# Measured durations in the planner's costs, gathered tiles in pieces of at most 512, and another first graph, in a four-layer graph network

## The chip, the cores and the metric

The kernel runs on one core of a Trainium2 chip. A core has TensorE (PE in the profile; PEld is its weight load), VectorE (DVE), ScalarE (ACT), GpSimd (POOL), and SyncE (SP), which issues transfers. The metric is the device time of one execution in microseconds; a kernel's time is the median of its runs. The profile is of one execution.

## The reference, cut to what matters

Sixteen graphs of 1024 nodes with 64 features, a dense weighted adjacency `adj` (16, 1024, 1024) with about nine entries per row, four layers, each with a norm ahead of it and a residual around it:

```python
def reference(x, adj, nodemask, ...):
    # each layer: h = max(layernorm(x), 0); x = x + layer(h)
    # layer 0: (adj @ h) @ W.T
    # layer 1: m = relu(relu(h @ W1 + b1) @ W2 + b2); msg = relu(adj @ m); GRU gates of (msg, h):
    #          (1 - z) * n + z * h
    # layer 2: T0 = h, T1 = adj @ T0, T2 = 2 * adj @ T1 - T0;  (T0*K0 + T1*K1 + T2*K2) @ weight + bias
    # layer 3: thin out the neighbour lists of nodes with more than 10 neighbours, both ways;
    #          agg = 0.25*quantile_0.25 + 0.5*quantile_0.5 + 0.25*quantile_0.75 over the neighbours,
    #          per feature (sort, then interpolate);  relu((h + agg) @ W1 + b1) @ W2 + b2, times the mask
```

## The kernel before

**Chains and the planner.** The work is written as generators, called chains, that yield one operation after another. `Weave.run` (line 430) is a list scheduler: of all chains it takes the operation that can start first by its reckoning, within 0.1 us the one of the chain with the smallest key, and issues it. The reckoning takes each operation's duration from `Line.cost` (line 304), a formula per engine. The order so found is kept on each engine by order dependencies, so an engine works its operations off in planned order, whatever really comes first. All operations of the chains are issued in line 301, so the profile's lines say L301 and are told apart by the names of their tiles.

**Chains and keys.** `transposing` loads the eight blocks (512 KB each) of a graph's adjacency by SP's queue, transposes them on PE into the tiles `AT` (15 of them, a stock shared by all graphs), key b - 2.5. The first eight blocks have places of their own: two tiles `block`, and six pieces of the two gather buffers `G`. `coding` (key b - 2) takes the sign of the transposed blocks on ACT into `there`, and PE multiplies it with fixed powers of two into `code`, 64 words per node that hold which neighbours there are. `listing` (key b - 1.5) first turns the node mask (a copy on DVE and a transposition on PE) and then unpacks each graph's code to a list of up to 24 neighbours per node, on DVE (`max`, `match_replace`, names `more`, `top`, `cand`, `L`). Two chains of `layering` (key b - 3) work even and odd graphs: `layers` computes layers 0 to 2. Layers aggregate with `into` (line 907: PE, `bank<-AT,nodes`, names of the tiles). Gates of layer 1 are products with `wg`; `of_h` and `hn` (lines 994 and 1012) are their steps on DVE. Layer 2 ends with a product with `wca` that is added to `X` (line 1058). Then `layers` waits for the list and writes a row per node into `pay`: list, counts, mask, and the last norm's features. SP stores them to `table` and `rows` in DRAM (lines 1075 and 1077).

**Norms.** `norm` (line 879) sums on DVE (`st`), squares on ACT per 128 nodes with an accumulator (`sq`, eight instructions, each with an instruction that reads the accumulator), takes the root on ACT (`sd`) and the reciprocal on DVE (`ri`), and scales on ACT per 128 nodes.

**Gathers and quantiles.** `gathering` (key b + 1) has POOL gather, per graph, 10 neighbour slots x 8 groups of 128 nodes = 80 indirect transfers (line 622) from `table` into a buffer `G`, 64 features and two numbers per row. There are two buffers `G`; a buffer is free again when PE has read the sorted slots for the quantiles. `quantiling` sorts on DVE: `hits` and `bad` find dropped neighbours, a `scalar_tensor_tensor` puts them at infinity, and a network of `min` and `max` sorts the 11 slots, partly into the tile `net`. Then `coef` weighs the slots, PE sums them (`bank<-G,c`), and `dense` does the last MLP (`yo`, `h`), key b. After all graphs, nodes with longer lists are gathered again in four groups (`MANY`, with up to 23 slots), at the end of the program.

**Width.** A slot of a graph has 8 x 64 = 512 elements per partition. `parts` (line 1147) cuts an operation over several slots in pieces of at most

```python
few = max(1, int(LONGEST / (T * C)))
```

slots, here two: 1024 elements. `coef`'s products take at most `few` slots as well (line 1218).

Of the kernel before, what the change touches and what calls it, by code (L numbers as in the profile page):

```python
# [16 lines left out]
AF = mybir.ActivationFunctionType  # L17
ALU = mybir.AluOpType
AX = mybir.AxisListType
# [3 lines left out]
P = 128  # L23
N = 1024
NT = N // P
# [76 lines left out]
GATHER = 1.33  # L102
RANK = 3.0
SHARE = 3
LONGEST = 1024
AT = 15
LIST_KEY = -1.5
CODE_KEY = -2
# [177 lines left out]
class Line:  # L286
# [15 lines left out]
        return op  # L302

    def cost(self, method, out, reads, kwargs):
        n = max(a.free_size() for a in [out] + reads)
        extra = "accum_out" in kwargs
        if self.name == "DVE":
            fixed = {"match_replace": 0.27, "max": 0.16}.get(method, 0.155)
            return fixed + n / 960 + 0.08 * extra, 0.0
        if self.name == "ACT":  # L310
            scalars = sum(hasattr(kwargs.get(k), "ap") for k in ("bias", "scale"))
            return 0.225 + n / 1400 + 0.09 * scalars + 0.19 * extra, 0.0
        if self.name == "PE":
            if method == "transpose":
                return 0.12, 0.25
            n = out.free_size()
            if n == NB and mybir.dt.size(reads[0].dtype) == 2:
                return 0.12, 0.3
            pair = n == 512 and reads[0].shape[0] == P and out.shape[0] == C
            return (0.46 if pair else max(0.22, 0.06 + n / 545)), 0.3  # L320
        if self.name == "SP":
            return 0.4, 2.0 + out.nbytes() / 150e3
        return 1.33, 2.2


class Weave:
# [16 lines left out]
    def give(self, name, t):  # L343
        self.stocks[name].append(t)
# [121 lines left out]
class Fast:  # L466
# [4 lines left out]
    def __init__(self, tc, half, whole, weights):  # L471
# [93 lines left out]
        self.weave = weave = Weave(tc)  # L565
        self.T, self.V, self.S = Line("PE", nc.tensor), Line("DVE", nc.vector), Line("ACT", nc.scalar)
        self.G, self.D = Line("POOL", nc.gpsimd), Line("SP", nc.sync)
        self.take = {}
        weave.leash = None, None

# [64 lines left out]
    def listing(self, nodemask):  # L635
        V = self.V
        mf, mu8 = self.small("h1", (P, 512))[:, 0:P], self.small("h1")[:, P:2 * P].bitcast(U8)[:, 0:P]
        yield self.D.dma_start(mu8, nodemask.rearrange("b (t p) -> (b t) p", p=P))
        yield V.tensor_copy(mf, mu8)
        bank = yield "q"  # L640
        yield self.T.transpose(bank[:, 0:P], mf, self.ident)
        self.mask = self.small("mask", (P, P))
        yield V.tensor_copy(self.mask, bank[:, 0:P])
        self.weave.give("q", bank)
        for b in range(GRAPHS):
            yield float(b) + LIST_KEY
            yield from self.lists(b)
        yield float(GRAPHS) - RANK
        yield from self.longest()

    def coding(self):

        V, T, S = self.V, self.T, self.S
        for b in range(GRAPHS):
            yield float(b) + CODE_KEY
            bank = yield "bits"
            yield T.matmul(bank.rearrange("p (t w) -> p t w", w=NB), self.ones16[0:1, 0:P],
                           self.low[0:1, None, :].to_broadcast([1, NT, NB]), start=True, stop=False)
            turned = self.turned[b]
            for j in range(0, NT, 2):  # L660
                there = yield "there"
                for i in range(2):
                    yield lambda: len(turned) > j + i
                    yield S.activation(there[:, i, :], turned[j + i], AF.Sign)
                self.masked[b] = j + 2
                own = there.rearrange("p i (t m) -> p (i t) m", m=P)[:, j:j + NT + 2:NT + 1, :]
                yield V.tensor_mul(own, own, self.noteye[:, None, :].to_broadcast([P, 2, P]))
                for i in range(2):
                    for t in range(NT):
                        yield T.matmul(bank[:, t * NB:(t + 1) * NB], there[:, i, t * P:(t + 1) * P],  # L670
                                       self.bits[:, (j + i) * NB:(j + i + 1) * NB], start=False,
                                       stop=j + i == NT - 1 and t == NT - 1)
                self.weave.give("there", there)
            code = yield "code"
            yield S.activation(code.rearrange("p t w -> p (t w)"), bank, AF.Copy, scale=1.0 / UNIT)
            self.weave.give("bits", bank)
            self.coded[b] = code
# [167 lines left out]
    def transposing(self, adj):  # L845

        D, T, S = self.D, self.T, self.S
        blocks = {}


        early = self.early

        def load(i):
            b, j = divmod(i, NT)
            blocks[i] = block = early.pop(0).rearrange("p (t m) -> p t m", m=P) if 2 <= i < NT else (yield "block")
            yield D.dma_start(block, adj[b, :, j * P:(j + 1) * P].rearrange("(t p) m -> p t m", p=P))

        total = GRAPHS * NT
        yield -1.0
        for i in range(NT):  # L860
            yield from load(i)
        for i in range(total):
            b, j = divmod(i, NT)
            yield float(b) - 2.5
            if NT <= i + 1 < total:
                yield from load(i + 1)
            block = blocks.pop(i)
            at = yield "AT"
            for half in range(2):
                bank = yield "tp"  # L870
                for q in range(4):
                    yield T.transpose(bank[:, q * P:(q + 1) * P], block[:, 4 * half + q, :], self.ident)
                yield S.activation(at[:, 512 * half:512 * half + 512], bank, AF.Copy)
                self.weave.give("tp", bank)
            if not 2 <= i < NT:
                self.weave.give("block", block)
            self.turned[b].append(at)

    def norm(self, w, h, X, then=None):

        V, S = self.V, self.S
        st, va, sd, ri, off = (self.small(f"{name}{w}") for name in ("st", "va", "sd", "ri", "off"))
        yield V.tensor_reduce(st, X, axis=AX.X, op=ALU.add)
        yield V.tensor_scalar(st, st, -1.0 / C, None, op0=ALU.mult)
        sq = self.small(f"sq{w}", (P, C))
        for t in range(NT):
            yield S.activation(sq, X[:, t, :], AF.Square, bias=st[:, t:t + 1], accum_out=va[:, t:t + 1])
        yield S.activation(sd, va, AF.Sqrt, bias=self.eps, scale=1.0 / C)
        yield V.reciprocal(ri, sd)
        yield V.tensor_mul(off, st, ri)  # L890
        for t in range(NT):
            yield S.activation(h[:, t, :], X[:, t, :], AF.Relu, bias=off[:, t:t + 1], scale=ri[:, t:t + 1])
            if then:
                yield from then(t)

    def layers(self, w, b, x):
# [10 lines left out]
        def into(bank, h, last=False):  # L907

            def step(j):
                if j == 0:  # L910
                    yield lambda: len(turned) > 0
                yield lambda: len(turned) > j
                for half in range(2):
                    yield T.matmul(bank[half * C:(half + 1) * C, :], h[:, j, :], turned[j][:, cols[half]],
                                   start=j == 0, stop=not last and j == NT - 1)
                if last:
                    yield lambda: self.masked[b] > j
                    give("AT", turned[j])
            return step
# [10 lines left out]

        h = yield "nodes"
        bank = yield "fm"
        yield from self.norm(w, h, X, into(bank, h))
        self.turns += 1
        wide = yield "wide"
        aggT = wide[0:C, :]
# [15 lines left out]
        def turn(t):  # L952
# [3 lines left out]
            if t % 4 == 3:  # L956
                yield S.activation(cat[0:C, cols[t // 4]], turned_h[-1][0:C, :], AF.Copy)
                give("fm", turned_h[-1])
        yield from self.norm(w, h, X, turn)
        aug = yield "wide"  # L960
        for half in range(2):
            bank = yield "fm"
# [57 lines left out]

        h = yield "nodes"
        bank = yield "fm"
        yield from self.norm(w, h, X, into(bank, h))
        wide = yield "wide"
        t1 = wide[0:C, :]
        for half in range(2):
# [21 lines left out]
                yield T.matmul(both[half * C:(half + 1) * C, t * P:(t + 1) * P], h[:, 4 * half + t, :], self.k02,  # L1048
                               start=False, stop=t == 3)
        give("nodes", h)  # L1050
        aug = yield "wide"
        for half in range(2):
            yield S.activation(aug[0:C, cols[half]], both[half * C:(half + 1) * C, :], AF.Copy)
        give("fm", both)
        bank = yield "fm"
        o = yield from by_node(bank, aug[0:C, :], self.wca, self.bcr)
        give("wide", aug)
        yield V.tensor_add(X, X, o)
        give("fm", bank)


        yield lambda: b in self.listed
        L, notes = self.listed[b]
# [6 lines left out]
                              op0=ALU.mult, op1=ALU.add)  # L1070
        give("L", L)
        give("notes", notes)
        yield from self.norm(w, pay[:, :, H:H + C], X)
        table = self.table[b * STRIDE:b * STRIDE + N, :].rearrange("(t p) c -> p t c", p=P)
        yield self.store(b, "table", table, pay[:, :, H:H + R])
        rows = self.rows[b * N:(b + 1) * N, :].rearrange("(t p) w -> p t w", p=P)
# [870 lines left out]
```

## Time and profile before

| | |
|---|---|
| median of 5 runs | 3383.01 us (3376.92 to 3401.72) |
| profiled execution | 3376.92 us, its span 3375.0 us |
| mean granted TensorE clock | 0.67 |
| instructions | 24102 |
| DMA | 141 MB, 42 GB/s over the span |
| gathers of line 622 | 1402, 997 ns each |
| first gather | 160.9 us |

The span runs from the first instruction to the last. In the views, L301 is a line, `G<-net` means that a tile `G` is written from a tile `net` (buffer numbers are left out), x is a count, and "idle before" is the time in which the engine stood still just before, with what released it ("remote" is a semaphore from elsewhere, "issue" a wait for nothing that the profile shows).

### The profile page before, as it was taken

The page shows a single profiled execution, that of the slowest core. Times are in us where ns is not written, and L with a number is a line of the kernel's source. Part 1 is how long each engine was busy: PE and PEld are TensorE (multiplying, and loading weights), DVE is VectorE, ACT ScalarE, POOL GpSimd, SP SyncE. Part 2 cuts the span into 40 slices and gives each one's busy share as a digit, 9 for nine tenths or more (in the row PEclk, how much of TensorE's full clock was granted, in tenths as well). Part 3 has the DMA queues.
Part 4 walks back from the last instruction along what each step waited for, and adds up shares of the span by engine and source line. Part 5 has one row for each costly group of instructions (what it writes and reads, how often), then busy time and mean ns, then how long its engine had stood idle before and what let it go on. Part 6 is the DMA issues. An engine that isn't in the chain of part 4 may idle for free. (4 is left out here: it accounts for less than half of the span.)

```text
span 3375.0 us, 24102 instructions
## 1 busy us (share of the span) xinstructions
PE 1744.6 (52%) x7024; PEld 803.7 (24%) x7024; DVE 1548.3 (46%) x3675; ACT 1093.9 (32%) x3002; POOL 1427.5 (42%) x1441
## 2 busy tenths in 40 slices
PE   6726455381746547273846645482745476333222
PEld 3302112130313223131413212230312232111121
DVE  2212136271725436171725436271725346395846
ACT  5504234260615234151614324260614234111100
POOL 1070624526061634526171534427071534527774
PEclk8858567595767667585767657585767677555555
DMA  3212222221212212222312212221211121111110
GB/s 84 60 27 53 45 46 50 37 62 25 63 31 54 46 30 62 31 51 30 76 26 47 44 32 50 39 65 26 67 26 39 42 38 25 19 21 27 26 29 16
DMA packets 246841, 141.00 MB, mean 42 GB/s; under 512 B 76048, under 2 KB 223952, under 8 KB 246704
## 3 DMA queue, kind: packets, MB, share of 16 engines
q1 hardware_dynamic: 199824, 90.21, 11.0%
q0 software_dynamic: 46096, 48.62, 10.1%
q8 instruction: 59, 0.97, 0.1%
q14 instruction: 78, 0.64, 0.1%
q10 hardware_dynamic: 784, 0.57, 0.1%
HBM read 120.12 MB, written 19.17 MB: 41 GB/s over the span
## 5 line engine op out<-in xcount | busy, mean ns | idle before, releaser
L622 POOL DMA_INDIRECT G<-table,pay x1402 | 1397.2, 997 | 1899.2 <-DVE net L301 1169.9
L301 PE MATMUL bank<-AT,nodes 128*64 128x512 f32 x2048 | 614.8, 683 | 116.1 <-issue 65.4
L301 PE MATMUL bank<-wide,wg 64*64 64x512 f32 (+1 forms) x192 | 119.6, 708 | 325.4 <-ACT wide L301 284.5
L301 PE MATMUL bank<-G,c 128*128 128x512 f32 (+3 forms) x382 | 196.0, 634 | 163.5 <-DVE G L301 98.5
L301 PEld LDWEIGHTS bank<-AT,nodes 128*64 128x64 f32 x2048 | 159.8, 153 | 421.9 <-issue 298.0
L301 PE MATMUL bank<-c,block 128*128 128x128 f32 x976 | 229.6, 365 | 18.9 <-ACT AT L301 8.1
L301 ACT ACTIVATE wide<-bank 64x512 f32<-64x512 f32 x128 | 75.6, 590 | 494.2 <-remote 362.2
L301 ACT ACTIVATE sq<-pay,st 128x64 f32<-128x64 f32 x512 | 177.7, 347 | 103.2 <-DVE st L301 87.4
L301 PE MATMUL bank<-of_h,m 64*128 64x512 f32 (+2 forms) x72 | 61.5, 949 | 284.8 <-issue 232.2
L301 DVE TENSOR_TENSOR hn<-nodes,bank 128x256 f32<-128x256 f32 x32 | 13.4, 419 | 421.4 <-remote 250.1
L301 ACT ACTIVATE AT<-bank 128x512 f32<-128x512 f32 x256 | 150.0, 589 | 158.7 <-PE bank L301 123.8
L301 DVE SCALAR_TENSOR_TENSOR of_h<-bank,bhn,wide 64x512 f32<-64x512 f32 x32 | 23.8, 744 | 382.0 <-PE bank L301 268.7
L301 DVE MAX8 L<-cand 128x8 f16<-128x103 f16 x384 | 92.3, 263 | 229.8 <-remote 136.2
L301 PEld LDWEIGHTS bank<-c,block 128*128 128x128 f32 x976 | 152.9, 187 | 169.3 <-issue 137.9
L301 DVE TENSOR_TENSOR G<-G 128x1024 f32<-128x1024 f32 (+7 forms) x215 | 187.4, 902 | 2.2
L301 PE MATMUL bank<-m,h 128*128 128x64 f32 x274 | 68.1, 407 | 218.6 <-ACT h L301 206.6
L301 ACT ACTIVATE nodes<-pay,off,ri 128x64 f32<-128x64 f32 x384 | 153.5, 429 | 24.1 <-DVE off L301 14.8
L301 DVE TENSOR_TENSOR net<-G 128x1024 f32<-128x1024 f32 (+7 forms) x140 | 140.3, 1032 | 3.2 <-PE bank L301 2.2
L301 PEld LDWEIGHTS bank<-G,c 128*128 128x128 f32 x382 | 72.6, 235 | 273.9 <-issue 154.7
L301 ACT ACTIVATE G<-G,coef 128x64 f32<-128x64 f32 x384 | 95.2, 337 | 128.3 <-DVE coef L301 128.2
L301 ACT ACTIVATE there<-AT 128x1024 f16<-128x1024 f32 x128 | 132.4, 1046 | 0.4
L301 PEld LDWEIGHTS bank<-m,h 128*128 128x128 f32 x274 | 59.1, 305 | 268.4 <-ACT h L301 219.3
(188 smaller groups left out, 2605.9 us busy)
## 6 DMA issues: line engine op xcount, KB each, us to landing
block<-in_adj SPq DMA_DIRECT2D x122, 512.0 KB
G<-table,pay POOLq DMA_INDIRECT x1402
rows<-pay SPq DMA_DIRECT2D x16, 632.0 KB
table<-pay SPq DMA_DIRECT2D x16, 264.0 KB
pay<-in_x SPq DMA_DIRECT2D x16, 256.0 KB
out<-yo SPq DMA_DIRECT2D x16, 256.0 KB
G<-in_adj SPq DMA_DIRECT2D x6, 512.0 KB
c<-in_half ACTq DMA_DIRECT2D x1, 246.0 KB
```

Of the source, the lines that this page charges most:

```text
L301: return Op(self, lambda: f(*args, **kwargs), writes, reads, cost, later)
L622: return self.nc.gpsimd.indirect_dma_start(out=out, out_offset=None, in_=table, in_offset=bass.IndirectOffsetOnAxis(ap=at, axis=0))
```

## The change

Four parts. (1) `Line.cost` gets other durations for PE and DVE, and a transfer has the same cost on every queue. The planner then finds another order for all engines. (2) `LONGEST` is 512: with graphs of 8 x 64 elements per slot, every operation on gathered tiles takes one slot. (3) For graph 0: `norm` has a form with five DVE operations over all 1024 nodes (`early`) in place of the squares and scalings on ACT; every second one of the first eight blocks is issued on ACT's queue (`self.A`); the mask's turn waits for graph 0's code, and coding for the end of graph 0's first aggregation (`self.turns > 0`). (4) For all graphs, the last product of layer 2 comes behind the list's columns of `pay`.

```diff
-LONGEST = 1024
+LONGEST = 512
...
     def cost(self, method, out, reads, kwargs):
+        if method == "dma_start":
+            return 0.4, 2.0 + out.nbytes() / 150e3
...
-            fixed = {"match_replace": 0.27, "max": 0.16}.get(method, 0.155)
+            fixed = {"match_replace": 0.145, "max": 0.155}.get(method, 0.155)
...
             if method == "transpose":
-                return 0.12, 0.25
+                return 0.19, 0.25
             n = out.free_size()
             if n == NB and mybir.dt.size(reads[0].dtype) == 2:
-                return 0.12, 0.3
+                return 0.075, 0.3
             pair = n == 512 and reads[0].shape[0] == P and out.shape[0] == C
-            return (0.46 if pair else max(0.22, 0.06 + n / 545)), 0.3
-        if self.name == "SP":
-            return 0.4, 2.0 + out.nbytes() / 150e3
+            return (0.58 if pair else max(0.34, 0.06 + n / 545)), 0.3
         return 1.33, 2.2
...
+        self.A = self.S
...
         yield self.D.dma_start(mu8, nodemask.rearrange("b (t p) -> (b t) p", p=P))
+        yield lambda: 0 in self.coded
         yield V.tensor_copy(mf, mu8)
...
             yield float(b) + CODE_KEY
+            yield lambda: self.turns > 0
             bank = yield "bits"
...
-            yield D.dma_start(block, adj[b, :, j * P:(j + 1) * P].rearrange("(t p) m -> p t m", p=P))
+            queue = self.A if i % 2 and i < NT else D
+            yield queue.dma_start(block, adj[b, :, j * P:(j + 1) * P].rearrange("(t p) m -> p t m", p=P))
...
-    def norm(self, w, h, X, then=None):
+    def norm(self, w, h, X, then=None, early=False):
...
+        if early:
+            yield V.tensor_add(h, X, st[:, :, None].to_broadcast([P, NT, C]))
+            square = yield "nodes"
+            yield V.tensor_mul(square, h, h)
+            yield V.tensor_reduce(va, square, axis=AX.X, op=ALU.add)
+            self.weave.give("nodes", square)
+            yield S.activation(sd, va, AF.Sqrt, bias=self.eps, scale=1.0 / C)
+            yield V.reciprocal(ri, sd)
+            yield V.scalar_tensor_tensor(h, h, 0.0, ri[:, :, None].to_broadcast([P, NT, C]), op0=ALU.max, op1=ALU.mult)
+            for t in range(NT):
+                if then:
+                    yield from then(t)
+            return
...
-        yield from self.norm(w, h, X, into(bank, h))
+        yield from self.norm(w, h, X, into(bank, h), early=b == 0)
...
-        aug = yield "wide"
-        for half in range(2):
-            yield S.activation(aug[0:C, cols[half]], both[half * C:(half + 1) * C, :], AF.Copy)
-        give("fm", both)
-        bank = yield "fm"
-        o = yield from by_node(bank, aug[0:C, :], self.wca, self.bcr)
-        give("wide", aug)
-        yield V.tensor_add(X, X, o)
-        give("fm", bank)
-
 
         yield lambda: b in self.listed
...
         give("L", L)
         give("notes", notes)
-        yield from self.norm(w, pay[:, :, H:H + C], X)
+
+        aug = yield "wide"
...
+        yield V.tensor_add(X, X, o)
+        give("fm", bank)
+
+
+        yield from self.norm(w, pay[:, :, H:H + C], X, early=b == 0)
```

The other calls of `norm` in `layers` get `early=b == 0` too.

More of the change, by code (lines that the diff above doesn't have):

```diff
@@ L958, in turn @@
                 give("fm", turned_h[-1])
-        yield from self.norm(w, h, X, turn)
+        yield from self.norm(w, h, X, turn, early=b == 0)
         aug = yield "wide"
@@ L1022, in layers @@
         bank = yield "fm"
-        yield from self.norm(w, h, X, into(bank, h))
+        yield from self.norm(w, h, X, into(bank, h), early=b == 0)
         wide = yield "wide"
@@ L1072, in layers @@
         give("notes", notes)
-        yield from self.norm(w, pay[:, :, H:H + C], X)
+        aug = yield "wide"
+        for half in range(2):
+            yield S.activation(aug[0:C, cols[half]], both[half * C:(half + 1) * C, :], AF.Copy)
+        give("fm", both)
+        bank = yield "fm"
+        o = yield from by_node(bank, aug[0:C, :], self.wca, self.bcr)
+        give("wide", aug)
+        yield V.tensor_add(X, X, o)
+        give("fm", bank)
+        yield from self.norm(w, pay[:, :, H:H + C], X, early=b == 0)
         table = self.table[b * STRIDE:b * STRIDE + N, :].rearrange("(t p) c -> p t c", p=P)
```

## The prediction

> **What bounds the kernel now.** I read the engines' busy times first, then the waits of POOL, then busy time by stretches, then the timelines inside one graph.
>
> ```profile
> PE 1744.6 (52%) x7024; PEld 803.7 (24%) x7024; DVE 1548.3 (46%) x3675; ACT 1093.9 (32%) x3002; POOL 1427.5 (42%) x1441
> ```
>
> No engine is over 52%, so the time is a chain of waits. POOL's gathers (line 622) come in streams of 80 per graph, which makes them a good clock:
>
> ```profile
> POOL G L622 <- DVE net L301: 1169.9, 15, 99.7
> POOL G L622 <- PE bank L301: 143.5, 16, 84.3
> POOL G L622 <- DMA table<-pay: 143.2, 1, 143.2
> ```
>
> POOL waits 1169.9 us in 15 pieces, some 80 us each, for DVE to finish an older graph's network, and once 143.2 us for the first table. From the timeline of POOL, the first gather is at 160.9 us, stream 2 starts at 544.5 and stream 15 at 3008.7: 13 cycles of 189.6 us on average. One cycle in detail, from 1487.3 (columns: start:end, length, busy us and count of PE, PEld, DVE, ACT, POOL, then clock, DMA share, GB/s):
>
> ```profile
> 1530.00:1550.00 20.00, 0.00 (x0) 0.00 (x0) 0.00 (x0) 0.00 (x0) 14.89 (x16) 0.50 0.15 27
> ...
> 1605.00:1676.00 71.00, 55.76 (x277) 27.32 (x277) 54.53 (x89) 50.23 (x138) 0.02 (x1) 0.76 0.30 66
> ```
>
> The reader is to see two limits. While gathers run (1487 to 1596), there are stretches where PE, DVE and ACT all stand still: hand-offs between them arrive late. Adding the gaps of 5 us and more over the whole span gives 583 us in 32 stretches. After the stream, DVE works through 71 us (54.5 busy, and 13 us in gaps of over 0.4 us, where it waits for ACT and PE; 9 us in the graph before), while POOL does nothing. Between the two lies the end of the gated unit of the next graph, `hn` (line 1012):
>
> ```profile
> 1554.88 1.21 ACT L301 ACTIVATE wide<-bank 64x512 f32<-64x512 f32 x2 [46.91 <-remote]
> ```
> ```profile
> 1601.57 0.42 DVE L301 TENSOR_TENSOR hn<-nodes,bank 128x256 f32<-128x256 f32 x1 [14.10 <-remote]
> ```
>
> The second half of `hn` follows at 1603.61, 116.3 us after the stream's start; over streams 2 to 13 it comes 113 to 120 after it, on average 117.6. Then the DVE phase runs to the next stream. So: cycle = time to `hn` + DVE phase.
>
> **First graph.** Durations are from the timelines of before. (a) PE stands still until 23.8, for the node mask:
>
> ```profile
> 23.79 0.48 PE L301 MATMUL bank<-c,h 128*128 128x128 f32 x1 [8.12 <-DVE h L301]
> ```
>
> The new wait moves the mask's copy and transposition behind graph 0's coding, and coding behind layer 0. From 24.06 to 51.4 PE transposes and aggregates eight blocks, 3.4 us each, 0.5 of it coding's eight small matmuls of 0.07, which now come later. From 15 us on, eight blocks at 2.9 are done at 38 rather than 51.4: -13. Ends: -8 (the hole alone) and -14. (b) Layer 1's norm: the eight squares with their accumulator reads and eight scalings on ACT keep the last `h` until 68.6, that is 12.7 us after the sum at 55.9; the new form is three DVE operations of 512 elements at 0.69, one more at 0.68, root 0.30 and reciprocal 0.20: 3.3 us, with hand-offs some 4: -9. (c) The same for layer 2, where PE needs some 11 us for the sixteen matmuls behind it: -7. (d) The same ahead of the table's store: -4. The sum is -33: the store, issued at 155.3, would be at 122 and the first gather at 128. Ends: -12 and -45.
>
> Behind the delayed coding waits the list, and behind the list the pay columns. In before, graph 0's list runs on DVE from 67 to 112, some 28 us of it at work, and the store is 43 us later. After's planned order puts it behind the first product of the gated unit: `hn` moves with (a) and (b) from 105 to some 83, the list with the norm in between needs 28 + 4 and ends at 115, pay columns and the last norm take 5 more: 120, just ahead of 122. I take no cost; the cover is 2 us thick, and beyond it each us of the list is a us of the store.
>
> Not all of -33 reaches the end. PE is busy 41.7 of the 42 us between 68 and 110, partly with graph 1. An earlier stream 0 freezes graph 1 at an earlier point of its chain, and stream 1 waits on exactly that chain (the 84.3 us above). I keep two thirds, -22; ends 0 and -40.
>
> (e) Half of the first blocks go to ACT's queue. The stretch shows what holds the loads:
>
> ```profile
> 0.00:24.00 24.00, 2.67 (x9) 1.44 (x10) 2.85 (x13) 6.99 (x20) 11.63 (x21) 1.00 0.88 216
> ```
> ```profile
> 2.86 14.87 SPq L301 DMA_DIRECT2D G<-in_adj  x6
> ```
>
> SP issues six blocks in 14.87 us, 2.48 each; 512 KB at 216 GB/s take 2.43. Issue goes at the speed of the transfers, which are at 0.88 of all DMA engines: gain nothing. The four issues on ACT could hold ACT for 3 x 2.48 = 7.4 us ahead of its first copies; it has little to do before 14 us. Taken: 0, ends 0 and +7. The Trainium skill speaks against this part: "DMA: Bandwidth & Descriptors", section "Issuing engines are not separate DMA queues", says that a second issuing engine saves only the sequencer's time for the issue. By this rule the gain would be at most the issue time.
>
> **512-wide operations.** By form, before has some 554 operations of 1024 elements on gathered tiles, 34.6 per graph, for instance
>
> ```profile
> L301 DVE TENSOR_TENSOR G<-G 128x1024 f32<-128x1024 f32 x97 | 117.4, 1220 | 1.0
> ...
> L301 DVE TENSOR_TENSOR G<-G 128x512 f32<-128x512 f32 x92 | 63.0, 685 | 0.5
> ```
>
> Busy means overlap, so I take starts. In DVE's timeline a 1024-wide operation follows another after 1.26 us where it reads its result (1667.05 to 1668.31) and after 1.14 where it doesn't (1668.31 to 1669.45); a 512-wide one is followed after 0.60 (1660.81 to 1661.41). Two halves cost 1.20: -0.06 or +0.06, so -2 to +2 us per graph. I take 0, the middle, since halves also separate dependent pairs. A gather beside these operations is slower: the first of stream 7 took 1.27, 1.43, 0.94, 1.20, 1.97 and 1.41 us against 0.94 later, together 2.6 us more than six of 0.94. I leave this unchanged, as DVE's busy time is. The skill's "SBUF — State Buffer", section "SBUF: two separate sides", describes, for the port pair that DVE and GpSimd share, an exclusive lock for a whole instruction; by it a gather would wait for half as long at most, which as an estimate would give 1.3 us per stream, 20 in all; the sum leaves it out.
>
> **Order of the chains.** By the planned order of after, DVE's work of one graph between the first `hn` and `coef` falls from 65.4 to 60.4 us (planned operations times the cadences above): a part of the list moves ahead of `hn`. Inside the stream DVE has room (28.7 us busy of 107 between 1300 and 1407), but a moved wait can also come late there; and 9 to 13 us of the phase are waits of DVE for ACT's roots and for PE that less filling work will uncover. I take half, -2.5; ends -9 (all gaps closed and nothing else) and +3.
>
> Against this: the planned layer-1 norm of the next graph now ends 0.4 us ahead of `coef`, not 13.6 us. Its transposes, both MLP steps, the aggregation and the gated unit are thus all in the stream, the gated unit some 30 us after its start, where hand-offs get late. Two rows bound that. In stream 1 nothing of the gated unit's second product could start until the stream had ended at 444.9:
>
> ```profile
> 457.90 2.07 PE L301 MATMUL bank<-wide,wg 128*128 128x512 f32 x2 [36.90 <-ACT wide L301]
> ...
> 479.69 0.42 DVE L301 TENSOR_TENSOR hn<-nodes,bank 128x256 f32<-128x256 f32 x1 [1.81 <-PE bank L301]
> ```
>
> That is `hn` at +135 (second half +137) and a cycle of 199.4. In stream 7 it started only at +68 and `hn` still came at +116, with a cycle of 188.7, with a 7.1 us pause of POOL at +62. In stream 3 it was through early and the cycle was 183.7. Nearest is stream 7, since most of the later chain still has the stream's second half: I take +1.5 against the mean, ends -4 and +20. The Chebyshev tail that is moved behind the pay columns changes places with about 1 us of small DVE work: 0 while the list is done earlier (it is, by 30 us of the phase); if it isn't, three products and an addition, 4 us, wait with it.
>
> **The sum.** 13 cycles x (-2.5 + 1.5) = -13; first graph -22; the wide tail after 3126 us has at most a dozen split operations, +1 at most, taken as 0. Together -35: 3376.9 becomes 3342 in an execution like the profiled one. That one was the fastest of five and stands 6 us under their median, so I forecast a median of 3348, own range 3310 to 3375.
>
> **Rivals.** (1) The gated unit is caught in the stream. For it: stream 1, and 583 us of standstill. Against it: the pauses of POOL, which remain as long as the third slot's gathers wait for PE. Place: from `hn` to the stream's end; price: stream 1's 199.4 against 189.6, 10 us x 13 = +130, less 22: +108, 3491. It decides from 1.7 us per cycle, where the first graph's gain is used up. (2) The chains fit better in every cycle, as in stream 3: -6 x 13 - 22 = -100, 3283. For it: the DVE phase has 9 to 13 us of waits; against it: 583 us of standstill that no durations in a plan describe. (3) The change does nothing to the end: the first graph's gain goes into a longer wait before stream 1, and the cycle keeps its 189.6: 3383.
>
> **Chances.** Forecast 0.40, rival 1 0.30, rival 2 0.18, rival 3 0.12. A measurement of this kernel tells 0.5%, 17 us, from nothing. Of the forecast's 0.40, 0.32 lie beyond that on the faster side, 0.05 within and 0.03 beyond it on the slower side; of rival 3, 0.03 go to the slower side: faster 0.32 + 0.18 = 0.50, same 0.05 + 0.09 = 0.14, slower 0.03 + 0.03 + 0.30 = 0.36. The range takes rival 2 with 40 us to spare and rival 1 up to 9 us per cycle (3383 - 22 + 117): 3240 to 3478.
>
> **What would show it.** First gather at 128, within 12. Second `hn` at +119 from a stream's start; above +125 on average means rival 1, below +112 rival 2. DVE phase (second `hn` to the next first gather) 69.5, from 72. Pairs of 512 within 0.1 us of one 1024. PE's wait of 8.12 at the mask gone. The forecast is wrong if POOL's pauses inside the streams vanish and standstill rises well over 583 us, or if stream 1's start moves by less than 10 us.

## The result, and the profile after

The changed kernel takes 3508.23 us (median of 10 runs, 3474.72 to 3519.69), the kernel before, beside it and earlier, 3388.55 (median of 17): a ratio of 1.034, 95% interval 1.031 to 1.037. It is slower by 3.4%, above the range. The profiled execution's span is 3491.5 us against 3375.0, 116.5 more. First the engines, then the waits of POOL, from the profile after:

```profile
PE 1773.2 (51%) x7024; PEld 787.1 (23%) x7024; DVE 1593.0 (46%) x4253; ACT 1062.2 (30%) x2905; POOL 1377.4 (39%) x1441
```
```profile
POOL G L623 <- DVE net L301: 1138.3, 14, 99.5
...
POOL G L623 <- DMA table<-pay: 89.7, 1, 89.7
...
POOL pay L623 <- DVE whom L301: 47.0, 1, 47.0
```

Still no engine binds. The wait for the networks is about what it was (1169.9 us before), the first table comes earlier, and a wait of 47 us for `whom`, the list of the nodes with many neighbours, is new. The starts of POOL's streams divide the 116.5 us:

| stretch | before | after | difference |
|---|---|---|---|
| to the first gather | 160.9 | 146.9 | -14.0 |
| stream 0 to stream 2 | 383.6 | 376.5 | -7.1 |
| stream 2 to stream 15 (13 cycles) | 2464.2 | 2515.9 | +51.7 |
| stream 15 to the end (the tail) | 366.3 | 452.2 | +85.9 |

Inside the cycles two large moves nearly cancel. Over streams 2 to 13 the second `hn` comes 136.0 us after a stream's start (before 117.5) and the DVE phase behind it lasts 57.6 us (before 72.0). One cycle of after, from 1311.1, in the timelines of ACT and DVE (start, length, engine, operation, count, and in brackets the idle time before it with its releaser):

```profile
1357.01 0.59 ACT L301 ACTIVATE wide<-bank 64x512 f32<-64x512 f32 x1 [19.50 <-remote]
1368.91 0.68 ACT L301 ACTIVATE wide<-bank,b1c 64x512 f32<-64x512 f32 x1 [10.11 <-remote]
1412.36 0.38 ACT L301 ACTIVATE nodes<-bank 128x256 f32<-128x256 f32 x1 [35.07 <-remote]
```
```profile
1448.77 0.42 DVE L301 TENSOR_TENSOR hn<-nodes,bank 128x256 f32<-128x256 f32 x1 [0.24 <-PE bank L301]
```

`wide<-bank,b1c` is the first MLP step of layer 1, `nodes<-bank` the second. In stream 7 of before both halves of the second were through at +14.3 and +17.2; here the steps wait in the stream and the second is through only after POOL stops issuing at 1401.8. Aggregation and gated unit come after that, and `hn` is at +137.7.

The tail, in DVE's timeline:

```profile
3113.99 0.42 DVE L301 TENSOR_TENSOR yo<-bank,pay 128x256 f32<-128x256 f32 x1 [44.87 <-remote]
...
3151.87 0.42 DVE L301 TENSOR_TENSOR yo<-bank,pay 128x256 f32<-128x256 f32 x1 [29.95 <-PE bank L301]
```

`yo` belongs to the last MLP of an older graph. In both kernels the plan puts these two into the middle of graph 14's network, with the last list's work (`whose`, then `whom`) partly behind them. In after they come 75 and 113 us into stream 15, for they wait out a standstill; in before the same two came 28 and 38 us into it, with hardly a wait. This is the first of them in before:

```profile
3036.80 0.42 DVE L301 TENSOR_TENSOR yo<-bank,pay 128x256 f32<-128x256 f32 x1 [1.03 <-issue]
```

All of DVE's gaps from stream 15 to the end add up to 126 us before and 204 after; its work there is 240 and 249. So the tail's 86 us are 78 of waiting and 8 of work.

What moved is the place where the late hand-offs begin. The first wait of stream 15 that ends with "remote" stands on ACT, 100 us into the stream in before and 25 us in after:

```profile
3108.66 0.59 ACT L301 ACTIVATE of_h<-bank 64x512 f32<-64x512 f32 x1 [8.93 <-remote]
```
```profile
3064.22 0.59 ACT L301 ACTIVATE of_h<-bank 64x512 f32<-64x512 f32 x1 [3.73 <-remote]
```

While DVE works on graph 14's network beside them, the first 24 gathers of stream 15 take 1.31 us each in before, with pieces of 1024, and 1.01 in after, with pieces of 512: POOL issues 15 and 19 of them in the first 25 us.

### The profile page after: what moved, and what is told of

The parts are those of the page before. It is cut to its first block, busy times and chain, and to the rows that moved or that the text cites. A ratio compares the mean times of both kernels' runs of the same rounds, so it can differ in the third digit from the quotient of the medians.

```text
span 3491.5 us, 24574 instructions
## 1 busy us (share of the span) xinstructions
PE 1773.2 (51%) x7024; PEld 787.1 (23%) x7024; DVE 1593.0 (46%) x4253; ACT 1062.2 (30%) x2905; POOL 1377.4 (39%) x1441
## 5 line engine op out<-in xcount | busy, mean ns | idle before, releaser
L623 POOL DMA_INDIRECT G<-table,pay x1402 | 1347.9, 961 | 2005.0 <-DVE net L301 1138.3
L301 PE MATMUL bank<-AT,nodes 128*64 128x512 f32 x2048 | 644.7, 689 | 635.6 <-ACT nodes L301 302.3
L301 PE MATMUL bank<-G,c 128*128 128x512 f32 (+3 forms) x382 | 212.1, 690 | 174.2 <-DVE G L301 152.4
L301 PE MATMUL bank<-wide,wg 64*64 64x512 f32 (+1 forms) x192 | 151.1, 886 | 251.4 <-ACT wide L301 247.7
L301 DVE TENSOR_TENSOR more<-more,top 128x64 f32<-128x64 f32 x80 | 17.6, 220 | 549.2 <-ACT sq L301 294.4
L301 DVE TENSOR_TENSOR G<-G 128x512 f32<-128x512 f32 (+3 forms) x313 | 195.0, 667 | 5.0 <-issue 1.7
L301 DVE TENSOR_TENSOR net<-G 128x512 f32<-128x512 f32 (+6 forms) x240 | 147.9, 664 | 5.0 <-remote 2.5
L301 ACT ACTIVATE G<-G,coef 128x64 f32<-128x64 f32 x384 | 104.0, 335 | 112.5 <-DVE coef L301 72.5
L301 PE MATMUL bank<-wide,w 64*64 64x512 f32 x64 | 49.1, 864 | 158.2 <-issue 130.3
L301 DVE MATCH_VALUE_LOAD cand<-L,cand 128x8 f16 x256 | 23.5, 92 | 214.0 <-remote 109.2
L301 DVE TENSOR_TENSOR G<-net 128x512 f32<-128x512 f32 (+7 forms) x189 | 115.2, 665 | 1.3 <-issue 0.4
```

The costliest lines, as they stand in the source:

```text
L301: return Op(self, lambda: f(*args, **kwargs), writes, reads, cost, later)
L623: return self.nc.gpsimd.indirect_dma_start(out=out, out_offset=None, in_=table, in_offset=bass.IndirectOffsetOnAxis(ap=at, axis=0))
```

## The experiments

The kernel before does not take the same time on every chip. The experiments ran in five groups, each on another chip; in two of them the kernel before took 2267 and 2253 us, in the others 3387 to 3402. Each kernel is compared with the kernel before of its own group. The ratios are of repeated runs; the other columns are from one profiled execution each: second `hn` and DVE phase are means over streams 2 to 13, cycle over 13. First the groups where the kernel before took 3387 to 3402:

| kernel | ratio, interval | first gather | second `hn` | DVE phase | cycle | tail |
|---|---|---|---|---|---|---|
| before | | 160.9 | 117.5 | 72.0 | 189.6 | 366 |
| after | 1.034, 1.031 to 1.037 | 146.9 | 136.0 | 57.6 | 193.5 | 452 |
| only_costs | 0.987, 0.983 to 0.991 | 155.5 | 128.6 | 58.4 | 186.1 | 365 |
| only_512 | 1.023, 1.019 to 1.026 | 161.8 | 115.4 | 72.5 | 188.3 | 465 |
| only_first | 0.965, 0.962 to 0.968 | 141.7 | 117.8 | 64.3 | 183.5 | 368 |
| only_moved | 1.001, 0.999 to 1.003 | 160.6 | 121.0 | 68.8 | 190.3 | 373 |
| no_512 | 0.995, 0.991 to 0.998 | 146.4 | 131.3 | 58.5 | 188.7 | 364 |
| slack11 | 1.000, 0.998 to 1.003 | 162.4 | 115.4 | 73.2 | 189.0 | 365 |
| first_paused | 0.807, 0.801 to 0.812 | 139.3 | 57.5 | 86.5 | 148.2 | 367 |
| after_paused | 0.872, 0.869 to 0.875 | 146.9 | 80.4 | 73.7 | 158.2 | 453 |
| each1_third | 0.939, 0.935 to 0.944 | 135.0 | 109.9 | 68.8 | 180.2 | 367 |
| after_tail_again | 1.023, 1.019 to 1.027 | 141.9 | 135.2 | 57.6 | 192.9 | 399 |

**One part at a time.** only_costs takes over `Line.cost` alone, only_512 the width, only_first the first graph (norms, queue, waits), only_moved the product of layer 2:

```diff
-LONGEST = 1024
+LONGEST = 512
```

> The kernel before with the new durations in the planner's costs alone. Theory A (the new order is what costs): second hn at +130 to +140 from a stream's start as in the changed kernel (before +118), DVE phase 57 to 62, the 13 cycles 193 on average, time 3430 to 3510. Rival B (512-wide pieces cost the time): cycle 189 to 190, time within 17 us of 3385. Rival C (any part that shifts the plan moves the time about as much): 3340 to 3480, no rule.

> The kernel before with pieces of at most 512 elements alone; durations in the plan as before. Theory A: the cycle stays within 2 us of 189.6 and the time within 30 us of 3385. Rival B: DVE phase longer by 3 us or more, time 3440 or more. Rival C: 3340 to 3480, and a cycle that goes with hn's place in the stream, not with DVE's busy time.

> The kernel before with the other first graph alone (norms on DVE, half of the first blocks on ACT's queue, mask and coding later). Theory A: first gather at 140 to 150 (before 160.9), cycles 189 to 191, time 3365 to 3390. Rival B: the same. Rival C: first gather the same, but the later cycles move with the plan: cycle 192 or more, or 187 or less, time beyond 3360 to 3400.

> The kernel before with the last product of layer 2 behind the pay columns alone. Theories A and B: cycle 189 to 191, time within 17 us of 3385. Rival C: cycle or tail moves by more than that although no operation was added: beyond 3365 to 3405.

No theory had the places. Rival C's bounds hold for three of the four times, but the moved product gives another order as well and moves nothing. The costs alone bring `hn` 11 us later and the DVE phase 14 us shorter, and gain. The pieces of 512 leave the cycle at 188.3 and lose 99 us in the tail. The first graph gains 117 us: in the profiled execution 19 at the first gather, but 78 in the cycles, although no operation of a later graph is changed by it; ten of its cycles are 180.8 to 181.4 long. Why is open; without hold-ups (below) its cycles gain nothing. The moved product changes nothing that is clear, though its single cycles run from 176 to 215. Singly the four give -49, +75, -117 and +1 us, together some -90; the whole change gives +120. The parts don't add up; that each works through the plan's order is the likely reason, and not shown.

The tail of only_512 has the same kind of waits as after, and its first "remote" wait stands 24 us into stream 15 too; what ended the waits of these two `yo` the profile does not show:

```profile
3099.56 0.42 DVE L301 TENSOR_TENSOR yo<-bank,pay 128x256 f32<-128x256 f32 x1 [48.41 <-issue]
...
3193.31 0.42 DVE L301 TENSOR_TENSOR yo<-bank,pay 128x256 f32<-128x256 f32 x1 [26.56 <-issue]
```

**The change without the width, and a jittered plan.** no_512 is the changed kernel with `LONGEST = 1024`. slack11 is the kernel before with another tolerance:

```diff
-SLACK = 0.1
+SLACK = 0.11
```

> The changed kernel with pieces of up to 1024 elements again, all else of the change kept. Theory T (the 512-wide pieces cost their time in the tail behind the last stream, 85 to 99 us there, by DVE's wait for yo; the other parts gain): tail 365 to 375, time 3260 to 3400. Rival U (the parts do not add up, the loss comes from their sum): tail 440 or more, or time above 3450.

> The kernel before with 0.11 instead of 0.10 as the planner's tolerance between chains: no operation and no cost changes, only some places in the order. If the plan's order alone is a lottery: time away from 3400 by 20 us or more, either way, with cycles of 181 to 196. If the order only matters where a cost is wrong: time within 17 us of 3400, cycle 189 to 191.

no_512 has its tail at 364 and its time at 3361: theory T holds. POOL issues 15 gathers in the first 25 us of stream 15, as in before, and the first "remote" wait comes at 101 us. Set beside after, the 512-wide pieces cost 88 us in the tail and, with the other costs in the plan, 4.8 us in each cycle, 63 in 13; as no_512's profiled execution is the fastest of its ten, 23 us under their median, the second figure is uncertain. slack11 says that a shifted plan is not a lottery of 20 us by itself: 1.000, cycle 189.0, though 1806 of the 3675 places in DVE's order hold another kind of operation.

**Pauses.** POOL fills a small tile ahead of every 16th gather; the planned order on PE, DVE and ACT is the same as without:

```diff
+    def pause(self):
+        for _ in range(PAUSES):
+            ins = self.nc.gpsimd.memset(self.idle, 0.0)
...
         def make():
+            if rest:
+                self.pause()
```

> The kernel with the other first graph alone, and ahead of every 16th gather of a stream (graphs 0 to 12) 24 small fills on POOL, some 4 to 6 us of pause; the planned order of PE, DVE and ACT is the same. Theory F (hand-offs between the other engines are held up by a long unbroken run of gathers, and a pause frees them): standstill under 300 us (without pauses 614), second hn at +60 to +100 instead of +117, cycles under 175, time under 3230. Rival G (the engines wait for something that the pauses do not touch): hn moves back by the pauses' 15 to 20 us, cycle 195 or more, time 3450 or more.

> The changed kernel with the same pauses. Theory F: second hn at +60 to +110 instead of +136, standstill under 300 us (502 without), cycles under 180, tail as in the changed kernel (452) for no pauses were put there, time 3250 to 3400. Rival G: cycle 205 or more, time 3600 or more.

POOL's timeline of first_paused shows a pause, DVE's the first `hn` of the stream that begins at 1417.9:

```profile
1438.10 6.56 POOL L624 MEMSET whose<- 128x144 f16 x24
```
```profile
1467.68 0.42 DVE L302 TENSOR_TENSOR hn<-nodes,bank 128x256 f32<-128x256 f32 x1 [3.22 <-remote]
```

`hn` is at +49.8, though four pauses of some 6.8 us, 27 in all, are put into each stream. Standstill (PE, DVE and ACT all idle for 5 us or more, with ACT's issuing of loads counted as work) falls from 614 to 152 us, and the time from 3286 to 2727. DVE and ACT work their operations off in the same order as in only_first. So the engines were held up by the gathers, not by work or by the plan. In after_paused standstill falls from 503 to 227, and `hn` stays 23 us behind that of first_paused: with the hold-ups mostly gone, the later place in the plan is what remains. Its tail, which has no pauses, is 453.

**Chips without hold-ups.** each1 has one fill ahead of each gather, short16 ten ahead of every 16th, all16 pauses in all streams up to the end, after_tail is the changed kernel with the old width in the tail:

```diff
-        few = max(1, int(LONGEST / (T * C)))
+        few = max(1, int((LONGEST if c.get("graph", GRAPHS) < GRAPHS - 2 else 1024) / (T * C)))
```

> The other first graph alone, with one small fill on POOL ahead of each gather of graphs 0 to 12 (0.27 us more per gather, no long pause). Theory R (a gather needs a little more time behind POOL than POOL needs to issue it, so a backlog grows; the mean distance counts): standstill under 250 us, second hn at +50 to +70, stream 118 to 128 long, cycle 125 to 138, time 2550 to 2720. Theory L (any long unbroken run of gathers holds the others up): second hn at +110 to +130, cycle 180 to 195, time 3250 to 3400.

> The other first graph alone, with 10 fills (about 2.9 us) instead of 24 ahead of every 16th gather of graphs 0 to 12. Theory R: 2.9 us per 16 gathers is 0.18 per gather, less than each1 has; if the backlog grows by less, the cycle is 126 to 135 and the time 2560 to 2700; if it grows by more, standstill comes back in part, 250 to 450 us, time 2750 to 3000. Theory L: as long as the breaks are there, hn stays at +50 to +60 and the cycle is 126 to 135.

> The other first graph alone, with pauses ahead of every 16th gather of all streams, the last graphs and the longer lists too; a pause is 48 fills of two elements, 4 to 7 us. The last two cycles (178 and 198 us with pauses up to graph 12 only) fall to 135 to 145, DVE's waits for yo in the tail (15 and 31 us) vanish, the tail falls from 366 to 320 to 350: time 2580 to 2680. If the hold-up were peculiar to the middle of the program, cycles and tail would stay as they were and the time within 30 us of 2727.

> The changed kernel with pieces of up to 1024 for the last two graphs and the longer lists, 512 for all others. Theory T (the narrow pieces cost their time in the tail alone, where the plan puts yo ahead of the last networks): tail 360 to 380 instead of 452, cycles 191 to 196 as before, time 3400 to 3440. Rival: the tail's loss comes from the state that the cycles leave behind: tail 430 or more, time above 3480.

The kernel before took 2267 us in this group. Beside it each1 is at 1.021 (1.015 to 1.028), short16 at 1.035 (1.028 to 1.042), all16 at 1.188 (1.181 to 1.195), after_tail at 0.990 (0.984 to 0.995). Nothing was held up, so pauses only cost, and none of the four could tell its theories apart. The next group has kernels once more, to see what the change is worth there:

> The kernel before itself, for its profile on this chip: ratio 0.995 to 1.005. If it takes about 2270, standstill is under 100 us (583 in the profile at the start), second hn at +40 to +65, cycles of 115 to 122.

> The changed kernel itself, once more, with a profile. Where the kernel before takes 3350 or more: ratio 1.03, second hn +130 to +140, tail 452. Where it takes about 2270 (no hold-ups): if the loss comes from hand-offs that are held up, second hn +55 to +65, tail 365 to 400, ratio 0.98 to 1.005; if it comes from the plan alone, tail 440 or more and ratio 1.03 or more.

> The other first graph alone, once more. Where the kernel before takes 3350 or more: ratio 0.960 to 0.970, as first measured (the plan is fixed, so the gain should repeat). Where it takes about 2270: first gather at 140, the cycles as in the kernel before, ratio 0.985 to 0.995.

> The same kernel as each1 (one small fill ahead of each gather of graphs 0 to 12), next to the kernel before on one chip. In the call of each1 the kernel before took 2267 instead of 3390 us, so nothing was held up there and nothing could be told. If this call's kernel before takes 3350 or more (hold-ups are there): theory R second hn at +25 to +70, cycle 120 to 130, 2300 to 2450; theory L second hn at +110 or more, 3200 or more. If it takes about 2270: 2300 to 2330.

The kernel before took 2253 us. These profiles are of that group:

| kernel | ratio, interval | first gather | second `hn` | DVE phase | cycle | tail |
|---|---|---|---|---|---|---|
| before_again | 1.001, 0.997 to 1.006 | 160.8 | 39.8 | 76.2 | 116.4 | 358 |
| after_again | 0.986, 0.980 to 0.993 | 146.7 | 57.0 | 58.1 | 115.6 | 343 |
| only_first_again | 0.987, 0.979 to 0.995 | 139.3 | 29.5 | 86.6 | 116.5 | 356 |
| each1_again | 1.025, 1.018 to 1.033 | 138.1 | 29.3 | 92.5 | 121.6 | 356 |

Here the changed kernel is 1.4% faster than the kernel before, and the tail with pieces of 512 is 15 us shorter, not 86 longer. 13 of the 15 are stream 15 itself, 104.3 us long rather than 117.2, as its gathers take 80 us rather than 93 beside DVE's work. A stretch of one stream of before_again (start:end, length, busy us and count of PE, PEld, DVE, ACT and POOL, then clock, DMA share and GB/s), and its first `hn`:

```profile
844.00:874.00 30.00, 30.00 (x81) 11.11 (x82) 17.57 (x74) 11.96 (x37) 20.91 (x21) 0.80 0.19 38
```
```profile
878.99 0.42 DVE L301 TENSOR_TENSOR hn<-nodes,bank 128x256 f32<-128x256 f32 x1 [0.31 <-PE bank L301]
```

PE is busy all of the 30 us in which POOL issues 21 gathers, and `hn` is at +34.8. Standstill is 62 us in the whole span, where the profile at the start had 583 with the same instructions.

**Two that were left.** The last group, beside a kernel before of 3387 us:

> One small fill ahead of each gather of graphs 0 to 12, over the other first graph. Only of use where the kernel before takes 3350 or more: theory R (mean distance of the gathers counts) second hn at +25 to +70, cycle 120 to 130, time 2300 to 2450; theory L (unbroken length counts) second hn at +110 or more, time 3200 or more; in between (hn +70 to +110, 2500 to 3000): both count. Where the kernel before takes about 2255: 2305 to 2320 again.

> The changed kernel with pieces of up to 1024 for the last two graphs and the longer lists. Where the kernel before takes 3350 or more: theory T (the narrow pieces cost their time in the tail alone) tail 360 to 380 instead of 452, time 3400 to 3440; rival (the tail's loss comes from where the hold-up falls, whatever the width): tail 430 or more, above 3480. Where it takes about 2255: 2235 to 2260 again.

each1_third is at 0.939 and its second `hn` at +110, near theory L. But the fill fell into the 0.3 us in which POOL stands between two gathers anyway; POOL's timeline:

```profile
1440.77 0.95 POOL L634 DMA_INDIRECT G<-table,pay  x1 [0.16 <-issue]
1441.72 0.24 POOL L624 MEMSET whose<- 128x144 f16 x1
1442.12 0.95 POOL L634 DMA_INDIRECT G<-table,pay  x1 [0.17 <-issue]
```

A gather follows another after 1.35 us rather than 1.25, not after 1.52 as expected. first_paused has 27 us more per stream, each1_third 8. Rate and unbroken length are therefore not told apart by these two. Stream 15 speaks for the rate, though no run varies it alone: all its 80 gathers come without a pause, and the late hand-offs begin 91 to 101 us into it with pieces of 1024 (before, no_512, after_tail_again), 24 and 25 us with pieces of 512 (only_512, after).

after_tail_again wins back 53 of the tail's 86 us (399) in its profiled execution and lands between its theories. That execution is the fastest of four; by the ratios, 1.034 and 1.023, the kernel gains 36 us. So the width in the tail is about half of that loss. The two `yo` come at 30 and 38 us again, but the two behind them, at 128 and 158 us, wait 48 and 30 us, where in before they waited 16 and 30; where the hold-up falls is the rest.

## Why the prediction was wrong

Of the sum's terms, the first graph's -22 came out as -21.1, the cycles' -13 as +51.7, and the tail's 0 as +85.9. The 3508 lies near the 3491 at which rival 1 was priced, but that is luck. Rival 1's place came true, with `hn` above +125; its price of +130 for the cycles did not, and the tail, which no rival had, made up the rest. Standstill, whose rise was to show the forecast wrong, fell from 583 to 503 us: what counted was where it fell. Three terms failed. Per cycle `hn` came 17 us later than the sum had it and the DVE phase was 12 us shorter, which leaves 65 us over the 13 cycles; the tail adds 86. The first graph was right in its sum alone.

- **"I take +1.5 against the mean, ends -4 and +20"** for `hn` in the stream. It was +18.5, close to the upper end. I had the cause, the gated unit pushed to some 30 us after the stream's start, and then took the nearest row, stream 7, where the unit started late and a pause of POOL let it through. In after the chain is held up one step earlier, at the MLP of layer 1. The delay is in the plan as much as in the chip: without hold-ups it is +17.2 (39.8 to 57.0).
- **"I take half, -2.5; ends -9 and +3"** for the DVE phase. It was -14.4, outside the ends, and -18.1 without hold-ups. I counted 5 us of planned work that moves ahead of `hn` and bounded the rest by 9 us of gaps. With costs alone (only_costs) the phase is 58.4 already, so the new order does it. Both effects that I had halved came in full: on average DVE's work in the phase falls from 57.3 to 48.7 us, as 9.8 us more of it is done ahead of `hn` in the stream, and its idle time in the phase falls from 14.7 to 8.9. `hn` and phase together are 189.5 before and 193.6 after, without hold-ups 116.0 and 115.1.
- **"The wide tail ... taken as 0".** It was +86, the largest term of the error. I counted split operations behind 3126 us, while the loss begins inside stream 15, and I had left the slowing of gathers beside wide operations "unchanged". It was that which changed: with pieces of 512 the gathers come closer together, the late hand-offs begin at 25 rather than 100 us, and they catch `yo` ahead of the rest of graph 14's network. Width and hold-ups together make the loss, as it is gone without either (no_512, 364; after_again, 343); that the gathers' distance is the link is read from five traces and not tested by itself.
- **First graph, -22 kept of -33.** -21.1 came of it (-14.0 and -7.1), but not by these steps, and the -7.1 need not be the first graph's: only_first has -19.2 and +1.7 there. (a) gave almost nothing: layer 0's aggregation ended at 49.9, not 38. It began at 20.6, not 15, and went at 3.5 us per block, not 2.9, so that taking coding's matmuls out saved nothing. (b) and (d) were right in kind: the norm of layer 1 is done at 58.6 rather than 68.6, `hn` comes 9 us earlier, and the store at 138.4 rather than 155.3.
- **(e), the queue: 0, ends 0 and +7.** PE began 5.6 us later than I had taken, which is near the upper end; no run has the queue alone. ACT's and PE's timelines of after:

```profile
7.86 9.85 ACTq L301 DMA_DIRECT2D G<-in_adj  x3
17.73 1.28 ACT L301 ACT_TABLE_LOAD   x1 [17.73 <-DMA G<-in_adj]
```
```profile
20.61 2.49 PE L301 MATMUL bank<-c,block 128*128 128x128 f32 x10 [9.62 <-DVE wg L546]
```

Three issues hold ACT for 9.85 us; the root for the first norm waits behind them, DVE waits for the root (9.17 us), and the copy of `wg` that PE waits for stands behind that on DVE. The wait of 8.12 us for the mask went away and one of 9.62 took its place. The Trainium skill's "DMA: Bandwidth & Descriptors", section "Issuing engines are not separate DMA queues", allows a gain of the issue time and calls that time usually small; here it is 3.3 us per issue of 512 KB, and it is ACT that pays it.

- **512-wide pieces.** Their cost on DVE was right: three 512-wide operations take 1.89 us (a row of after at 3158.03), 0.60 from start to start, and only_512's cycle moves by -1.3 us. The effect beside the gathers was there: a gather takes 967 ns in only_512 against 997, 42 us of POOL's time in all, and without hold-ups 987 (after_again) against 1099 (before_again). Per stream of 80 that is 2.4 and 9 us, where my estimate had 1.3. That agrees with the Trainium skill's "SBUF — State Buffer", section "SBUF: two separate sides", whose lock for a whole instruction I had left out of the sum. The cycles gained nothing from it that can be seen; in the tail it gained 13 us without hold-ups, and with them it seems to have brought the hold-up forward.

Without the tail's 86 us the time would have been some 3422, inside the range but still slower than before.

## What to carry to other kernels

Where engines work in a planned order, one late hand-off holds everything behind it in the same queue, so an edit has to be followed at every place where the program leaves its steady state, the end above all, and not in one middle cycle. An operation that gets out of another engine's way also changes that engine's pace: here the faster gathers went with a gain of 13 us in the last stream where nothing was held up, and with a loss of 86 in the tail where they held up the others. Of two known rows for a step, the nearest in timing was the wrong choice: ask which of them has the relief (here POOL's pause) that the changed order will still have. And a gain or loss of a few per cent through an order can have the other sign on another chip: this change is 1.034 where gathers hold up the others and 0.986 where they don't. only_first is faster than before on both (0.965 and 0.987), and first_paused is at 0.807 where there are hold-ups.

## What the runs showed of the hardware

Two kinds of chips, or of conditions on them, run the same instructions in 2253 and 3388 us. DVE's and ACT's operations take equally long on both, as does the middle gather (0.944 and 0.945 us; the mean gather takes 0.997 and 1.099). The mean granted clock is 0.67 on the slow one and 0.76 on the other, but PE's busy time differs by 95 us only, of the 1123 between the spans. What differs is that with streams of gathers under way a result of PE reaches ACT or DVE 10 to 50 us late. This is how the view of waits in the profile of before lists the largest such group (total, number, longest):

```profile
ACT wide L301 <- remote: 460.4, 17, 75.2
```

In all it has 49 waits of ACT (1091 us) and 132 of DVE (551 us) that end with "remote"; before_again has none. It is the signal that is late, not the next engine: PE ends the products that ACT's step at 1554.88 needs at 1513.50, the semaphore that carries the news to ACT shows no update between 1501.53 and 1554.86, and ACT starts 0.02 us behind that one. DVE's signals to itself are late too: between 1510 and 1529 us its chain of `max` and `match_replace` for `L` stands still for 0.5 to 2.5 us ahead of nearly every dependent step, where between 1562 and 1568 us it runs without a gap.

Pauses of some 7 us on POOL after every 16 gathers brought the ratio from 0.965 to 0.807; where nothing is held up, pauses in all streams cost 19%. What makes the difference between the chips stays open, and so does whether it is the rate of the gathers or their unbroken length that matters, although stream 15 points to the rate.
